# A transformer block in exact fp32: one round of norms and transposes placed ahead of its products, and the last block's attention output gathered in one place

## The chip, the cores and the metric

The kernel runs on one core of a Trainium2 chip. The metric is device time in microseconds for one launch; lower is better. TensorE (PE in the profile) multiplies, VectorE (DVE) and ScalarE (ACT) do the elementwise work, GpSimd (POOL) a few small operations, and SyncE (SP) issues most of the DMAs.

## The reference

The input is x of 2048 rows and 1024 columns. Everything is fp32.

```python
h   = layernorm(x)
q, k, v = split(h @ Wqkv + bqkv, 3)            # 256 columns each
out = softmax(q @ k.T / 16) @ v                 # one head over all 2048 rows
x   = x + layernorm(out @ Wo + bo)
h   = layernorm(x)
x   = x + layernorm((silu(h @ W_gate.T) * (h @ W_up.T)) @ W_down.T)   # inner width 2752
```

## The kernel before, in words

**Numbers.** Every fp32 operand of a large product is split into two rounded parts, hi (made by ScalarE) and lo (the rest, made by VectorE), and a product is three matmuls: hi by hi, hi by lo, lo by hi. `mm3` at L142 to L144 issues these three. `split` at L109 (ScalarE, hi) and L110 (VectorE, lo) makes the parts.

**Rows.** The 2048 rows are 16 blocks of 128 rows, numbered 0 to 15, in four groups of four. A block is loaded into one of four tiles `xin` (block t into tile t modulo 4, `load_x`, L160). `prep1` then takes the mean and variance (`norm_stats`: L116, L119 and L120 on VectorE, L121 on GpSimd), norms the rows (L127, VectorE), and turns them with eight 128-column transposes on TensorE (L135) into two PSUM banks, from where `split` writes hi and lo. Only then may the tile be loaded with the block four further on; that load is the last statement of `prep1`.

**Stage 1, products.** For each group g, `qk(g, i)` makes two slices of k (i = 0, 1) and two of q (i = 2, 3) with 24 matmuls each, in banks 4 and 5, and `v_block(g, tb)` makes 128 rows of v with eight pairs of matmuls of 512 and 256 columns (L189, L190), in bank 6 or 7. A `v_block` ends with two VectorE adds that read its bank (L193, L194) and a `split` of the result; the next but one `v_block` reuses the bank. Group 0 and the norms of blocks 4 to 7 have a hand-written order. From group 1 on the order of statements is only a wish: the program is built by a scheduler that plans every engine's order from the traced statements, their data dependencies and estimated costs, and engines run their own list in that fixed order. A few statements (`keep_in_program_order`) must stay in the traced order, among them the statistics of blocks 8 to 11. In the kernel before, `prep1` of block 8+i is traced behind `qk(1, i)`.

**Stage 2, attention.** For each block i of 128 queries: `turn` transposes the softmax weights (L396), `attend(i)` multiplies them with v, `turn_o` transposes the result (L415) and splits it (L417, L418), `proj` multiplies with Wo (12 matmuls of `mm3`, in banks 5 and 7, each bank read by L428), and `xpose` and `residual` do the second norm of an earlier block. `attend` keeps hi and lo of v side by side, so one matmul of 512 columns (L404) gives both hi by hi (left half of bank 6) and hi by lo (right half), and one of 256 columns (L405) adds lo by hi to the right half. ScalarE copies the left half out (L407), and VectorE adds the right half to the copy (L408).

**The seam.** While the last block, 15, is in attention, the feed-forward stage has begun: its products (L761) and the splits of its weights and inputs (L563, L564, L109, L110, L540, L775, on ScalarE and VectorE) are mixed in, the block's result lies in the tile `xe`, and `proj(15)` is the last of the attention. In the feed-forward stage TensorE takes weights from slots that ScalarE and VectorE refill as TensorE frees them.

Of the kernel before, what the change touches and what calls it, by code (L numbers as in the profile page):

```python
# [18 lines left out]
D = 256  # L19
F = 2752  # L20
NT = T // P
NC_ = C // P
G = 512
NG = T // G
TB = G // P
FB = F // P
FR = F - FB * P
NKB = T // P
# [6 lines left out]
def block_kernel(ctx, tc, x, wqk, wv, bqk, bv, wo, bo, wgu, wlast, wd, out):  # L35
# [12 lines left out]
    nc = tc.nc  # L48
# [4 lines left out]
    def tl(p, shape, dt, name):  # L53
        return p.tile(shape, dt, tag=name, name=name, bufs=1)
# [22 lines left out]
    bank = [tl(bank_pool, [P, 512], F32, f"bank{i}") for i in range(8)]  # L77
# [27 lines left out]
    def f32(ap):  # L105
        return ap.bitcast(F32)
# [17 lines left out]
    def norm_rows(t, pin):  # L124

        m, r, _ = norm_stats([t[:, 0:512], t[:, 512:1024]], pin)
        nc.vector.tensor_scalar(t, t, m, r, ALU.subtract, ALU.mult)  # L127

    def transpose_rows(t, dst, tb, banks):

        for hf in range(2):
            b = banks[hf]
            for j in range(4):
                cb = 4 * hf + j
                nc.tensor.transpose(b[:, j * P : (j + 1) * P], t[:, cb * P : (cb + 1) * P], ident)  # L135
            src = b.rearrange("p (j t) -> p j t", j=4)
            cols = slice(tb * P, (tb + 1) * P)
            split(dst[:, 4 * hf : 4 * hf + 4, 0, cols], dst[:, 4 * hf : 4 * hf + 4, 1, cols], src)

    def mm3(o, w, m, first, last, pin=lambda i: i):  # L140

        pin(nc.tensor.matmul(o, w[0], m[0], start=first, stop=False))  # L142
        pin(nc.tensor.matmul(o, w[0], m[1], start=False, stop=False))  # L143
        return pin(nc.tensor.matmul(o, w[1], m[0], start=False, stop=last))  # L144


    def kT(d, g):
        return slot(kx, 4 * d + g)

    vt = a1.rearrange("p a b c -> p (a b c)").rearrange("p (k h d) -> p k h d", h=2, d=D)  # L150
# [8 lines left out]
    def load_x(t):  # L159
        nc.sync.dma_start(xin[t % TB], x[t * P : (t + 1) * P, :])  # L160
# [3 lines left out]
    def prep1(t, banks):  # L164

        r = xin[t % TB]
        norm_rows(r, tc.keep_in_program_order if t < 3 * TB else None)
        transpose_rows(r, xT[(t // TB) % 2], t % TB, banks)
        if t + TB < NT:
            load_x(t + TB)  # L170

    def qk(g, i, b, pin=lambda i: i):
        xg = xT[g % 2]
        for c in range(8):
            mm3(b, (wqk_s[i][:, c, 0, :], wqk_s[i][:, c, 1, :]), (xg[:, c, 0, :], xg[:, c, 1, :]), c == 0, c == 7, pin)
        if i < 2 or g == 0:
            dst = kT(i, g) if i < 2 else qa[:, i - 2, :, :]
            pin(nc.scalar.activation(dst[:, 0, :], b, AF.Identity, bias=bqk_s[:, i : i + 1]))
            pin(nc.vector.scalar_tensor_tensor(dst[:, 1, :], b, bqk_s[:, i : i + 1], f32(dst[:, 0, :]), ALU.add, ALU.subtract))
        else:  # L180
            s = qst[i % 2]
            nc.scalar.activation(s, b, AF.Identity, bias=bqk_s[:, i : i + 1])
            nc.sync.dma_start(q_d[g][:, i - 2, :], s)

    def v_block(g, tb, b):
        xg = xT[g % 2]
        cols = slice(tb * P, (tb + 1) * P)
        for c in range(8):
            nc.tensor.matmul(b, xg[:, c, 0, cols], wv_s[:, c, :, :].rearrange("p a f -> p (a f)"), start=(c == 0), stop=False)  # L189
            nc.tensor.matmul(b[:, D:], xg[:, c, 1, cols], wv_s[:, c, 0, :], start=False, stop=(c == 7))  # L190
        k = g * TB + tb
        s = vst[tb % 2]
        nc.vector.tensor_tensor(s, b[:, :D], bv_s, ALU.add)  # L193
        nc.vector.tensor_tensor(s, b[:, D:], s, ALU.add)  # L194
        split(vt[:, k, 0, :], vt[:, k, 1, :], s)
# [168 lines left out]
    def o_of(i):  # L364

        return o_s[i % 2] if i < NT - 1 else xe[:, 0:D]
# [33 lines left out]
    def attend(i):  # L400
        b = bank[6]
        p = pT[i % 2]
        for k in range(NKB):
            nc.tensor.matmul(b, p[:, k, 0, :], vt[:, k, :, :].rearrange("p h d -> p (h d)"), start=(k == 0), stop=False)  # L404
            nc.tensor.matmul(b[:, D:], p[:, k, 1, :], vt[:, k, 0, :], start=False, stop=(k == NKB - 1))  # L405
        o = o_of(i)
        nc.scalar.copy(o, b[:, :D])  # L407
        nc.vector.tensor_tensor(o, b[:, D:], o, ALU.add)  # L408

# [55 lines left out]
    qk(0, 3, vb[3], pin)  # L465
    for g in range(1, NG):
        for i in range(4):
            qk(g, i, bank[4 + i % 2])
            if g + 1 < NG:
                prep1((g + 1) * TB + i, (bank[2 * (i % 2)], bank[2 * (i % 2) + 1]))  # L470
        if 0 < g < NG - 1:
            for tb in range(TB):
                v_block(g, tb, bank[6 + tb % 2])
# [588 lines left out]
    for i in range(NT):  # L1062
# [26 lines left out]
        if i > 0:  # L1089
            turn_o(i - 1)  # L1090
        attend(i)
        if i > 0:
            proj(i - 1)
# [126 lines left out]
```

## Time and profile before

| what | value |
|---|---|
| time, median of 3 runs | 1691.93 us (1691.12 to 1692.08) |
| the profiled execution: its own time | 1693.37 us |
| the profiled execution: span in the trace | 1691.6 us |
| TensorE busy | 1669.9 us, 99% of the span |
| VectorE busy | 1097.4 us, 65% |
| ScalarE busy | 700.8 us, 41% |
| GpSimd busy | 94.1 us, 6% |
| mean granted TensorE clock | 0.996 of full speed |

The span starts with the first instruction and ends with the last; the profiled execution's own time has 1.8 us more around it. The profile's waits give, for an instruction that found its engine idle, what released it: engine, line and tile waited for, total time, number of waits, longest wait. The chain of waits follows the last instruction back to what released it, step by step. The table of windows gives each engine's busy time in a stretch and, under PEclk, the share of its full clock that TensorE was granted there.

### The profile page before, as it was taken

Reading aid. Unit: us, or ns where it says so; the run is one execution under the profiler, and the core shown is the slowest. Engines: PE = TensorE matmul, PEld = TensorE weight load, DVE = VectorE, ACT = ScalarE, POOL = GpSimd, SP = SyncE. Lnnn points to the kernel's source line nnn. Section 1 sums busy time; section 2 is a strip of 40 time slices with the busy share of each in tenths; the row PEclk is TensorE's granted clock in tenths of the full one; section 3 lists DMA queues with packets and bytes.
Section 4 is the critical chain, followed back from the end, with each engine's and each line's share of the span. In section 5 each row is a group of like instructions: output and inputs, shape, how many; then the busy total and the mean of one; then the engine's idle time right before and its main releaser. Section 6 shows DMA issues by size and latency. Waiting matters only on the chain.

```text
span 1691.6 us, 21210 instructions
## 1 busy us (share of the span) xinstructions
PE 1669.9 (99%) x7821; PEld 1391.9 (82%) x7821; DVE 1097.4 (65%) x1676; ACT 700.8 (41%) x1043; POOL 94.1 (6%) x121
## 2 busy tenths in 40 slices
PE   9999999999999999999999999999999999999997
PEld 8888887888788888888888888888888888888886
DVE  7552667667787777776578457966555665455458
ACT  4222455544544444444355444433333333344343
POOL 1000000000001111111000000100000000000001
PEclk9999999999999999999999999999999999999999
DMA  6221023334646566666567666533322223576664
GB/s 214 72 72 57 26 88 117 99 116 174 219 166 210 197 216 228 218 210 219 175 213 249 213 192 203 199 118 119 129 102 94 94 94 125 215 217 197 191 192 159
DMA packets 131016, 271.02 MB, mean 160 GB/s; under 512 B 13280, under 2 KB 29792, under 8 KB 130912
## 3 DMA queue, kind: packets, MB, share of 16 engines
q1 hardware_dynamic: 129472, 266.52, 47.5%
q10 hardware_dynamic: 1440, 3.15, 0.5%
q8 instruction: 61, 1.00, 0.3%
q14 instruction: 43, 0.35, 0.1%
HBM read 185.73 MB, written 83.89 MB: 159 GB/s over the span
## 4 chain that ended last, share of the span: by engine, by line
PE 95%; DVE 2%; DMA 1%; issue 1%; ACT 1%; POOL 0%; POOLq 0%; SPq 0%; DVEq 0%; ACTq 0%
PE bank L761 71%; PE bank L142 4%; PE bank L143 4%; PE bank L144 4%; PE bank L404 3%; PE bank L405 2%; PE bank L396 1%; PE bank L189 1%; PE bank L503 1%; DMA f<-x 1%; PE bank L190 1%; PE bank L274 1%; DVE a L110 0%; PE bank L135 0%; PE bank L945 0%
## 5 line engine op out<-in xcount | busy, mean ns | idle before, releaser
L761 PE MATMUL bank<-a 128*128 128x512 f32 x1164 | 274.2, 389 | 0.0
L761 PEld LDWEIGHTS bank<-a 128*128 128x128 f32 x1164 | 218.5, 188 | 45.4
L761 PE MATMUL bank<-xb,a 128*128 128x512 f32 x912 | 212.3, 389 | 0.4 <-DVE a L110 0.4
L761 PEld LDWEIGHTS bank<-xb,a 128*128 128x128 f32 x912 | 171.0, 188 | 36.3 <-DVE a L110 0.8
L110 DVE TENSOR_TENSOR a<-f2p,a 128x1024 fp32r<-128x1024 f32 (+2 forms) x133 | 134.8, 1013 | 58.5 <-ACT a L109 54.5
L109 ACT CAST a<-f2p 128x1024 fp32r<-128x1024 f32 (+2 forms) x133 | 117.7, 885 | 128.6 <-PE bank L761 104.2
L110 DVE TENSOR_TENSOR a<-f,a 128x1024 fp32r<-128x1024 f32 (+2 forms) x87 | 89.8, 1033 | 113.5 <-ACT a L109 111.5
L761 PE MATMUL bank<-wvo 128*128 128x512 f32 x612 | 149.6, 389 | 0.0
L761 PE MATMUL bank<-kx,a 128*128 128x512 f32 x612 | 145.9, 389 | 0.0
L761 PE MATMUL bank<-a,a 128*128 128x512 f32 x588 | 139.6, 389 | 0.0
L761 PEld LDWEIGHTS bank<-wvo 128*128 128x128 f32 x612 | 114.9, 188 | 23.9
L761 PEld LDWEIGHTS bank<-kx,a 128*128 128x128 f32 x612 | 114.9, 188 | 23.8
L761 PEld LDWEIGHTS bank<-a,a 128*128 128x128 f32 x588 | 110.4, 188 | 22.9
L109 ACT CAST a<-f 128x1024 fp32r<-128x1024 f32 (+2 forms) x87 | 68.1, 783 | 125.1 <-PE bank L761 104.5
L775 DVE TENSOR_TENSOR p_s<-bank,p_s 128x512 f32<-128x512 f32 x96 | 65.2, 682 | 76.6 <-PE bank L761 42.4
L761 PE MATMUL bank<-a,wvo 128*128 128x512 f32 x444 | 106.0, 389 | 0.0
L761 PE MATMUL bank<-kx,wvo 128*128 128x512 f32 x420 | 100.1, 389 | 0.0
L404 PE MATMUL bank<-a,a 128*128 128x512 f32 x256 | 94.8, 403 | 2.8 <-ACT f L505 2.0
L761 PEld LDWEIGHTS bank<-a,wvo 128*128 128x128 f32 x444 | 83.3, 188 | 17.3
L110 DVE TENSOR_TENSOR wvo<-f,wvo 128x1024 fp32r<-128x1024 f32 (+1 forms) x51 | 59.6, 1169 | 55.8 <-ACT wvo L109 55.6
L761 PEld LDWEIGHTS bank<-kx,wvo 128*128 128x128 f32 x420 | 78.8, 188 | 16.4
L121 POOL TENSOR_TENSOR small<-small,mhalf 128x1 f32<-128x1 f32 x48 | 38.7, 808 | 697.2 <-DVE small L120 668.6
(267 smaller groups left out, 2782.4 us busy)
## 6 DMA issues: line engine op xcount, KB each, us to landing
f2p<-wgu SPq DMA_DIRECT2D x41, 512.0 KB, 5.2
f<-x SPq DMA_DIRECT2D x30, 512.0 KB, 3.8
hd_S<-p_s SPq DMA_DIRECT2D x60, 256.0 KB, 4.6
f<-wgu SPq DMA_DIRECT2D x22, 512.0 KB, 3.5
wr<-wgu SPq DMA_DIRECT2D x21, 512.0 KB, 5.7
f<-wd SPq DMA_DIRECT2D x20, 512.0 KB, 4.7
hd_A<-xi SPq DMA_DIRECT2D x40, 256.0 KB, 2.0
td_T<-f SPq DMA_DIRECT2D x40, 256.0 KB, 4.5
```

Source lines behind the costliest of these rows:

```text
L109: nc.scalar.copy(hi, src)
L110: (lo_engine or nc.vector).tensor_tensor(lo, src, f32(hi), ALU.subtract)
L121: nc.gpsimd.tensor_tensor(s[:, 15:16], s[:, 14:15], mhalf, ALU.pow)
L142: pin(nc.tensor.matmul(o, w[0], m[0], start=first, stop=False))
L143: pin(nc.tensor.matmul(o, w[0], m[1], start=False, stop=False))
L144: return pin(nc.tensor.matmul(o, w[1], m[0], start=False, stop=last))
L189: nc.tensor.matmul(b, xg[:, c, 0, cols], wv_s[:, c, :, :].rearrange("p a f -> p (a f)"), start=(c == 0), stop=False)
L190: nc.tensor.matmul(b[:, D:], xg[:, c, 1, cols], wv_s[:, c, 0, :], start=False, stop=(c == 7))
L404: nc.tensor.matmul(b, p[:, k, 0, :], vt[:, k, :, :].rearrange("p h d -> p (h d)"), start=(k == 0), stop=False)
L405: nc.tensor.matmul(b[:, D:], p[:, k, 1, :], vt[:, k, 0, :], start=False, stop=(k == NKB - 1))
L761: one = nc.tensor.matmul(o, w[i], m[j], start=first and n == 0, stop=last and n == 2, skip_group_check=chained)
L775: nc.vector.tensor_tensor(o, a, b, op)
```

## The change

Two parts. First, in group 1 alone, `prep1` of blocks 8 to 11 is traced in front of `qk(1, i)` and not behind it; in group 2, `prep1` of blocks 12 to 15 stays behind `qk(2, i)`. Second, `attend` of block 15 runs the three parts as three matmuls of 256 columns, all added up in the left half of bank 6, so that ScalarE's copy is the whole result and no VectorE add follows. The other 15 blocks keep the old form.

```diff
     def attend(i):
         b = bank[6]
         p = pT[i % 2]
+        o = o_of(i)
+        if i == NT - 1:
+
+            for k in range(NKB):
+                for j, (h, l) in enumerate(((0, 0), (0, 1), (1, 0))):
+                    nc.tensor.matmul(b[:, :D], p[:, k, h, :], vt[:, k, l, :], start=(k == 0 and j == 0), stop=(k == NKB - 1 and j == 2))
+            nc.scalar.copy(o, b[:, :D])
+            return
         for k in range(NKB):
             nc.tensor.matmul(b, p[:, k, 0, :], vt[:, k, :, :].rearrange("p h d -> p (h d)"), start=(k == 0), stop=False)
             nc.tensor.matmul(b[:, D:], p[:, k, 1, :], vt[:, k, 0, :], start=False, stop=(k == NKB - 1))
-        o = o_of(i)
         nc.scalar.copy(o, b[:, :D])
         nc.vector.tensor_tensor(o, b[:, D:], o, ALU.add)
...
     for g in range(1, NG):
         for i in range(4):
+            if g == 1:
+                prep1(2 * TB + i, (bank[2 * (i % 2)], bank[2 * (i % 2) + 1]))
             qk(g, i, bank[4 + i % 2])
-            if g + 1 < NG:
-                prep1((g + 1) * TB + i, (bank[2 * (i % 2)], bank[2 * (i % 2) + 1]))
+            if g == 2:
+                prep1(3 * TB + i, (bank[2 * (i % 2)], bank[2 * (i % 2) + 1]))
         if 0 < g < NG - 1:
             for tb in range(TB):
                 v_block(g, tb, bank[6 + tb % 2])
```

Here `NT` is 16, `NKB` 16, `NG` 4, `TB` 4 and `D` 256. Line numbers in the text are those of the kernel before.

## The prediction

> **What bounds the kernel now.** I read the shares first, then TensorE's waits, then the windows for the clock, then the chain around each wait.
>
> ```profile
> PE 1669.9 (99%) x7821; PEld 1391.9 (82%) x7821; DVE 1097.4 (65%) x1676; ACT 700.8 (41%) x1043; POOL 94.1 (6%) x121
> ```
>
> TensorE sets the end: it idles 21.7 us in all (1691.6 − 1669.9). So a change can win idle time, or time at a lowered clock, but hardly more. TensorE's longest waits:
>
> ```profile
> PE bank L415 <- DVE xe L408: 3.3, 1, 3.3
> PE bank L135 <- DVE f L127: 2.2, 1, 2.2
> PE bank L404 <- ACT f L505: 2.0, 2, 1.4
> ```
>
> The first lies at the seam, the second in stage 1: the two places that the diff touches. Behind 450 us the waits add up to only 0.4 us, so what is won there reaches the end. The windows around these waits show a second price:
>
> ```profile
> 99.00:105.00 6.00, 5.61 (x27) 5.14 (x28) 3.18 (x7) 1.58 (x3) 0.00 (x0) 0.72 0.26 90
> ...
> 262.00:278.00 16.00, 14.57 (x82) 12.22 (x80) 11.29 (x24) 8.21 (x15) 1.63 (x4) 1.00 0.35 92
> ...
> 442.00:450.00 8.00, 7.09 (x25) 5.74 (x26) 5.95 (x9) 4.33 (x6) 0.00 (x0) 0.79 0.93 315
> ```
>
> The clock share falls only here: 0.28 × 6 = 1.68 and 0.21 × 8 = 1.68 us lost, that is 3.4 us at half speed behind each wait. The 1.4 us wait in the middle row cost no clock.
>
> Stage 1, the chain of waits:
>
> ```profile
> 90.75 3.76 DMA f<-x
> 94.54 1.29 DVE small L116 x2
> ...
> 98.61 0.73 DVE f L127
> 99.39 1.97 PE bank L135 x8
> ```
>
> Block 11's transposes (99.39) wait for its norm. Its statistics ran at 92.20, but a little behind them block 14's sat at the head of VectorE's queue until 94.54 for a load issued at 90.75, when block 10's transposes freed the tile. From 99.39 to 102.82 TensorE did eight transposes (0.87) and five matmuls of `v_block` (3 × 0.235 + 2 × 0.115), 1.81 us of work in 3.43. The wait costs 2.19 + 1.62 = **3.8 us**.
>
> The seam, in the timeline:
>
> ```profile
> 439.24 0.39 PE L144 MATMUL bank<-wvo,oTs 128*128 128x512 f32 x1
> 439.54 0.36 ACT L407 COPY xe<-bank 128x256 f32<-128x256 f32 x1
> ...
> 442.44 0.42 DVE L408 TENSOR_TENSOR xe<-bank,xe 128x256 f32<-128x256 f32 x1
> ...
> 442.91 0.44 PE L415 MATMUL bank<-ident,xe 128*128 128x128 f32 x2 [3.29 <-DVE xe L408]
> ```
>
> ScalarE's copy is done at 439.90; the add starts 2.54 us later, because VectorE has feed-forward splits and sums back to back ahead of it.
>
> **What the Trainium skill says.** "TensorE: Matmul & The Clock Gate", section "What's actually happening": the clock is halved or full, judged in a free-running window of 3413 ns. The two losses of 3.4 us at half clock agree. The same page, "Why this matters for your kernels", asks for no idle gap over about 3 us; here 2.19 us sufficed, and 1.4 us did not, and between these I take a chance. "Perfetto Trace Analysis", section "Tensor Engine Instruction (MATMUL, LD_WEIGHTS)": ScalarE and VectorE queues are strictly first in, first out; the 2.54 us of the ready add agree. "TensorE: Matmul & The Clock Gate", "Back-to-back issue gap": spacing is set by weight load and matmul together; for my 256-column matmuls the trace has a row of its own, below.
>
> **Part 1, the moved `prep1`.** I compared both kernels' built instruction orders, engine by engine. Nothing is added or removed. Block 8's transposes move from behind the 14th matmul of `qk(1,2)` to behind that of `qk(1,1)`, block 9's from `qk(1,3)` into `qk(1,2)`, block 10's from behind `v_block(2,0)` to before the last pair of `v_block(1,2)`. With 0.227 us per 512-column matmul, 0.35 per `v_block` pair and 0.87 per eight transposes, I place the new order on the trace:
> - Block 8 at 64.34 + 14 × 0.227 = 67.5 (73.0 before), block 9 at 73.0 (79.1). `qk(1,3)` ends at 82.6 as before; 3 pairs, then block 10 at 83.7 (89.7).
> - Block 14's load goes out 1.06 us behind block 10's start, as before: 84.7; landing takes 3.79 to its reader: 88.5 (94.5 before).
> - TensorE: block 10's transposes, the last pair of `v_block(1,2)`, `v_block(1,3)`, block 12's transposes, `v_block(2,0)` reach 91.35. There `v_block(2,1)` needs bank 7, which `v_block(1,3)` filled and VectorE must have read (L194).
> - VectorE's new order has block 14's statistics ahead of that read: 88.52 + statistics 1.20 + L193 0.33 + L119 0.11 + split 0.60 + split 0.33 + L119 0.11 + split 0.60 + L194 0.42 = 92.22.
>
> So a **new wait of 0.9 us** comes at 91.35; behind it stand `v_block(2,1)`, `v_block(2,2)` and block 11's transposes, which then come at 97.5, 3.4 us after their norm (94.1), and no longer wait. The clock should hold, as it did at 1.4 us. Won: 3.8 − 0.9 = **2.9 us**. If the load takes 0.5 us more or less, the wait follows it by as much until VectorE's earlier work (done 88.1) sets it: at least 0.5.
>
> The rest of part 1 costs nothing, for these covers: GpSimd's powers (0.55 us) come as often, with the engine 6% busy. On SP, the loads of blocks 12, 13 and 14 pass before the q stores and the read-back of q (L369 at 85.62), which VectorE takes up only at 133.3; if that cover were gone, a store's 2 us would appear there. `v_block(3,0)` moves back from 101 to about 153, but the orders are the same again from block 2's `attend` (about 219) on. TensorE's waits between 105 and 219 sum to 1.5 us (0.7, 0.5 and 0.3, for ScalarE, VectorE, ScalarE). I take no change, with bounds of −1.5 and +1.5.
>
> **Part 2, block 15.** TensorE runs 48 matmuls of 256 columns for 16 pairs. Stage 1 has such matmuls, each behind its own weight load:
>
> ```profile
> 15.46 2.87 PE bank L274 x24
> ```
>
> 0.12 us each, so 5.76 for 16 × 0.35 = 5.60: +0.16 us. The add (0.33 of VectorE's time) goes. L415 follows the copy: 439.95, not 442.91. Next come two transposes (0.22) and six products (1.37), to 441.55. Then `proj(15)` must have bank 7, which L428 reads for `proj(14)`, and L428 stands in VectorE's queue where it stood, less the add: 442.77 − 0.33 + 0.75 = 443.19. The stall is not gone; **what is late next is L428**, and TensorE waits 1.65 us there, `proj(15)` and all feed-forward products behind it. The third matmul needs L418, done 443.52, in time. `proj(15)` runs 443.22 to 445.95 at full clock; before, the products behind it began at 448.90. Won: **2.95 us**, of which 1.6 is clock. The +0.16 is hidden behind VectorE's queue; without that cover it is paid. Bounds: if 1.65 us of idling costs the clock, 1.7 less; if VectorE is less behind, up to 1.6 more.
>
> **Sum.** 2.9 + 2.95 = 5.9 us off the profiled execution: span 1685.7, own time 1687.5. The median of the runs is 1.4 below that own time, so 1691.93 − 5.9 = 1686.0.
>
> **Rivals.**
> - *The clock still drops at the seam.* 1.65 us is 48% of a window, and with part of the 0.5 us ahead of it up to 2.0 us (59%) can fall into one; 1.4 us (41%) was safe, 2.19 us (64%) was not. 5.9 − 1.7 = 4.2: 1687.7.
> - *The wait in stage 1 only changes place.* Block 14's load lands 1.3 us later (it now runs with the q stores): 2.2 us of idling and a clock drop take part 1 whole. Then 1689.0. Against it: the loads issued at 74.05, 80.19 and 90.75 were in their readers' hands 3.5 to 3.8 us later.
> - *Slower.* The same wait at `v_block(2,1)`, VectorE held at its head by block 14's load. The change loses once wait and clock exceed the 6.75 us of 3.8 and 2.95, a wait of 5.1 us, a load 4.2 us late. At 8 us late, 1695.8. For it: two q stores, the read-back and the load crowd into 83 to 89 us. Against it: DMA was busy for only 0.41 of 75 to 90 with nearly the same transfers.
> - *The change does nothing*, the scheduler keeping its order: excluded by the built orders.
> - *More than computed*: the waits of 105 to 219 go too: 1684.5.
>
> **How the numbers follow.** A measurement can tell 0.2% (3.4 us) from no change. As computed 0.5 (1686.0, own range 1684.8 to 1687.2), clock drop at the seam 0.25 (1687.7), wait moved 0.13 (1689.0, within 0.2%), more 0.07, slower 0.05, of which 0.01 stays within 0.2%. Faster 0.5 + 0.25 + 0.07 = 0.82, same 0.14, slower 0.04. Range 1684.2 to 1689.6: the extra gain below, the moved wait above.
>
> **What would show it.** In the changed profile: no wait of L135 for L127; one of about 0.9 us of L189 for L194 near 91; L415 waiting under 0.6 us for ScalarE's copy; the first matmul of `proj(15)` waiting about 1.7 us for L428 or L418; PEclk at 1.00 near 99 and 442. I am wrong if the waits behind 105 us grow by more than 2, or the feed-forward stage shows new ones.

## The result, and the profile after

| kernel | median of its runs | ratio to the kernel before, 95% interval |
|---|---|---|
| before | 1692.03 us (14 runs) | |
| changed | 1688.33 us (1686.61 to 1689.32, 14 runs) | 0.9977 [0.9970, 0.9984] |

The change makes the kernel 3.7 us faster. The forecast said 1686.0, that is 5.9 us. The profiled execution of the changed kernel took 1688.38 us of its own time, with a span of 1686.6.

Line numbers below are those of each run's own kernel. In the changed kernel they are 7 to 9 higher than before: L435 is the old L428 (the read of a `proj` bank), L437 the store of `proj`'s result, L594 the old L585 (loads of feed-forward inputs), L676 the load of weights, L770 the old L761 (feed-forward products), and L831 the old L822, ScalarE's copy of a feed-forward bank into the tile `xi`. L422 and L425 are the old L415 and L418 (block 15's transposes and the split of their result), L572 and L573 the old L563 and L564 (input splits), and L408 is the new line of block 15's 256-column matmuls.

The shares, after:

```profile
PE 1666.8 (99%) x7837; PEld 1389.7 (82%) x7837; DVE 1096.0 (65%) x1675; ACT 698.8 (41%) x1043; POOL 93.7 (6%) x121
```

TensorE is busy for 3.1 us less than in the first profile and idle for 19.8 us instead of 21.7. The busy time that went is the lowered clock, which the windows over the two old places show as gone (the columns are the stretch, its length, busy time of PE, PEld, DVE, ACT and POOL, then PEclk, the DMA share and GB/s):

```profile
99.00:105.00 6.00, 6.00 (x29) 4.97 (x28) 5.21 (x12) 1.21 (x3) 0.55 (x1) 1.00 0.29 90
...
442.00:450.00 8.00, 8.00 (x37) 6.61 (x36) 3.47 (x4) 2.36 (x3) 0.00 (x0) 1.00 0.81 287
```

TensorE's waits, after:

```profile
PE bank L142 <- DVE f L435: 1.5, 1, 1.5
...
PE bank L770 <- ACT xi L831: 1.4, 1, 1.4
...
PE bank L189 <- DVE small L120: 0.4, 1, 0.4
```

Neither the 3.3 us nor the 2.2 us of before is there. The first and third lines are the waits that the forecast put in their place. (For the third it named L194. The profile names L120, which VectorE runs directly behind L194: L194 ended at 91.68, and TensorE went on at 91.83.) The second line is a wait for which the forecast had no price: it lies at 457 us, in the feed-forward stage.

The seam in TensorE's timeline (start, duration, line and operation; the bracket gives the idle time ahead and what ended it):

```profile
433.37 1.35 PE L408 MATMUL bank<-a,a 128*128 128x256 f32 x10
434.56 0.40 PE L142 MATMUL bank<-wvo,oTs 128*128 128x512 f32 x1
...
436.03 0.44 PE L422 MATMUL bank<-ident,xe 128*128 128x128 f32 x2
...
439.41 0.47 PE L142 MATMUL bank<-wvo,oTs 128*128 128x512 f32 x1 [1.53 <-DVE f L435]
...
442.25 1.52 PE L770 MATMUL bank<-qa,a 128*128 128x512 f32 x6
```

Ten 256-column matmuls take 1.19 us, so 0.119 each. The transposes of the result (L422) start with no wait. The products behind `proj(15)` start at 442.25 instead of 448.90: 6.65 us ahead, of which only 5.0 us are left at the end of the span. The chain of waits behind the seam shows where the rest went (start, duration, what):

```profile
438.60 0.66 DVE f L435
...
439.29 7.60 DMA at_d<-f
...
446.91 0.32 SPq L594
...
447.80 5.04 DMA f<-wgu
...
456.74 0.58 ACT xi L831
...
457.37 2.83 PE bank L770 x11
```

VectorE writes `proj(14)` into the tile f4[0] (L435). Its store takes 7.6 us to land. At the head of SP's queue an input load into the same tile (L594) waits for that store, and the weights' load stands behind it in the queue. ScalarE splits these weights when they land (452.94), then, in its own order, runs one more split of weights and two of inputs, and only then copies the bank that TensorE needs. TensorE became free sooner than this chain.

### The profile page after: what moved, and what is told of

It is laid out like the page before. It is cut to its first block, busy times and chain, and to the rows that moved or that the text cites. A ratio compares the mean times of both kernels' runs of the same rounds, so it can differ in the third digit from the quotient of the medians.

```text
span 1686.6 us, 21240 instructions
## 1 busy us (share of the span) xinstructions
PE 1666.8 (99%) x7837; PEld 1389.7 (82%) x7837; DVE 1096.0 (65%) x1675; ACT 698.8 (41%) x1043; POOL 93.7 (6%) x121
## 4 chain that ended last, share of the span: by engine, by line
PE 93%; DMA 2%; DVE 2%; ACT 1%; issue 1%; POOL 0%; SPq 0%; POOLq 0%; DVEq 0%; ACTq 0%
PE bank L770 70%; PE bank L142 4%; PE bank L143 4%; PE bank L144 4%; PE bank L412 3%; PE bank L413 2%; PE bank L396 1%; PE bank L189 1%; PE bank L512 1%; DMA f<-x 1%; PE bank L274 1%; PE bank L190 1%; DMA out<-bo_s 0%; DMA at_d<-f 0%; DVE a L110 0%
## 5 line engine op out<-in xcount | busy, mean ns | idle before, releaser
L770 PE MATMUL bank<-a 128*128 128x512 f32 x1164 | 274.3, 389 | 0.0
L770 PEld LDWEIGHTS bank<-a 128*128 128x128 f32 x1164 | 218.6, 188 | 45.3
L770 PE MATMUL bank<-xb,a 128*128 128x512 f32 x912 | 212.5, 390 | 0.4 <-DVE a L110 0.4
L770 PEld LDWEIGHTS bank<-xb,a 128*128 128x128 f32 x912 | 171.0, 188 | 36.1 <-DVE a L110 0.8
L110 DVE TENSOR_TENSOR a<-f2p,a 128x1024 fp32r<-128x1024 f32 (+2 forms) x133 | 134.7, 1012 | 58.1 <-ACT a L109 51.2
L109 ACT CAST a<-f2p 128x1024 fp32r<-128x1024 f32 (+2 forms) x133 | 117.5, 883 | 129.2 <-PE bank L770 104.7
L110 DVE TENSOR_TENSOR a<-f,a 128x1024 fp32r<-128x1024 f32 (+2 forms) x87 | 89.7, 1031 | 112.7 <-ACT a L109 110.7
L770 PE MATMUL bank<-wvo 128*128 128x512 f32 x612 | 149.6, 389 | 0.0
L770 PE MATMUL bank<-kx,a 128*128 128x512 f32 x612 | 145.9, 389 | 0.0
L770 PE MATMUL bank<-a,a 128*128 128x512 f32 x588 | 139.8, 390 | 1.4 <-ACT xi L831 1.4
L770 PEld LDWEIGHTS bank<-wvo 128*128 128x128 f32 x612 | 114.9, 188 | 23.8
L770 PEld LDWEIGHTS bank<-kx,a 128*128 128x128 f32 x612 | 114.9, 188 | 23.8
L770 PEld LDWEIGHTS bank<-a,a 128*128 128x128 f32 x588 | 110.3, 188 | 24.6 <-ACT xi L831 1.8
L109 ACT CAST a<-f 128x1024 fp32r<-128x1024 f32 (+2 forms) x87 | 67.9, 780 | 129.7 <-PE bank L770 106.2
L770 PE MATMUL bank<-a,wvo 128*128 128x512 f32 x444 | 106.0, 389 | 0.0
L770 PE MATMUL bank<-kx,wvo 128*128 128x512 f32 x420 | 100.1, 389 | 0.0
L770 PEld LDWEIGHTS bank<-a,wvo 128*128 128x128 f32 x444 | 83.4, 188 | 17.3
L110 DVE TENSOR_TENSOR wvo<-f,wvo 128x1024 fp32r<-128x1024 f32 (+1 forms) x51 | 59.6, 1168 | 55.8 <-ACT wvo L109 55.7
L770 PEld LDWEIGHTS bank<-kx,wvo 128*128 128x128 f32 x420 | 78.8, 188 | 16.3
L412 PE MATMUL bank<-a,a 128*128 128x512 f32 x240 | 88.8, 403 | 2.8 <-ACT f L514 2.1
```

The costliest lines, as they stand in the source:

```text
L109: nc.scalar.copy(hi, src)
L110: (lo_engine or nc.vector).tensor_tensor(lo, src, f32(hi), ALU.subtract)
L770: one = nc.tensor.matmul(o, w[i], m[j], start=first and n == 0, stop=last and n == 2, skip_group_check=chained)
```

## The experiments

Two theories at the start. **T:** this chain of transfers caps what the seam can win. **R:** each part fell short by itself. The kernel before ran beside every group of variants; its medians were 1692.19, 1691.85 and 1692.36 us. The groups ran on different chips, so variants of different groups are compared only roughly, to about 0.5 us.

### The changed kernel again

> The changed kernel once more, for a second profiled execution beside the variants on one chip: 1688.3 by every theory. If the waits of the first trace are systematic, the wait for the copy of xi is 1.0 to 1.7 us again and the one at the first matmul of proj(15) 1.4 to 1.7 us; if they are chance, they are not.

Measured: 1688.56 us, 0.9980 [0.9972, 0.9988]. Both waits came back, the one for L435 with 1.3 us, the one for the copy of `xi` with 0.9, both a little under the ranges given. The chain was the same. In this execution the store landed in 6.3 us instead of 7.6 and the weights' load went out at 446.79, 1.0 us sooner, but took 0.9 us longer to land. So the copy was done only 0.13 us sooner, and most of the shorter wait is TensorE's coming 0.28 us later.

### Each part alone

Part 1 alone drops the new branch in `attend`. Part 2 alone puts `prep1` back behind `qk`.

> Part 1 alone: the moved norms and transposes, block 15's attention output in its old form. Theory T (a chain of transfers behind the seam caps what part 2 wins): part 1 carries most of the gain of 3.7 us, so 2.9 to 3.2 us below the kernel before, about 1689.0; no wait for the norm near 99 us, a wait of 0.4 us for VectorE's read of a bank near 91, and the old wait of 3.3 us at the seam with TensorE's clock lowered there. Rival R (both parts fell short alike, each worth about six tenths of its forecast): 1.8 us below, about 1690.2.

> Part 2 alone: block 15's output as 48 products of 256 columns in one place, stage 1 as before. T: the seam's wait shrinks to about 1.5 us and the clock holds there, but a wait of 1 to 1.5 us for ScalarE's copy of xi comes in the feed-forward stage, because the weights' load goes out behind the store of block 14 as before; 0.5 to 1 us below the kernel before, about 1691.3. R (each part worth six tenths of its forecast): 1.8 us below, about 1690.2, and the wait in the feed-forward stage has another cause. The forecast's own sum: 2.95 us below, about 1689.1.

Measured: part 1 alone 1690.75 us, ratio 0.9988 [0.9982, 0.9995], 1.4 us below before by the medians (2.0 by the ratio). Part 2 alone 1690.84 us, 0.9992 [0.9986, 0.9999], 1.35 us below. T missed part 1 by half, and R's number was closer there; for part 2 the measured gain lies between T's 0.5 to 1 and R's 1.8. The intervals, about 1.1 us to either side, don't tell whether the parts add up to the 3.7 us of both together. The windows of the two profiles show one reason for the smaller gain of part 1. Part 1 alone, over the seam:

```profile
430.00:455.00 25.00, 21.46 (x92) 17.47 (x91) 15.27 (x19) 10.97 (x16) 0.00 (x0) 0.93 0.79 273
```

Part 2 alone, over stage 1's old wait and over the seam:

```profile
96.00:103.00 7.00, 5.08 (x34) 4.31 (x33) 5.58 (x14) 2.37 (x5) 1.06 (x2) 1.00 0.43 148
...
430.00:455.00 25.00, 22.83 (x113) 18.81 (x113) 16.10 (x20) 11.39 (x17) 0.00 (x0) 1.00 0.84 295
```

The second fence is the point: the old wait of stage 1 is still there (TensorE idle for 1.92 of 7 us), but the clock held at 1.00. The 1.62 us of lowered clock that the forecast counted at this place are paid in some executions only. Both profiles also show the wait for ScalarE's copy of `xi` in the feed-forward stage, 0.6 us in part 1 alone and 1.0 in part 2 alone. In part 2 alone its chain runs through the store of block 14 and the blocked load, as in the changed kernel. In part 1 alone it does not: the blocked load was out at 445.96, and the weights' load went out at 447.39, when VectorE had read the old weights out of the same tile (L110, done at 447.37).

### The clock: a second profile of before

> A second profiled execution of the kernel before. If both losses of clock in its first profile are systematic, the granted clock is lowered near 99 us and near 444 us again. If the loss at a wait of 2 us depends on how the wait falls into the clock's windows, this execution may show one of them or none: by the clocks of the runs so far, that near 444 us in about three of four executions, that near 99 us in about one of three. Where the clock holds near 99, the five products of v_block behind the wait take 1.8 us, not 3.4.

Measured: 1692.12 us. TensorE's waits in the two places:

```profile
PE bank L135 <- DVE f L127: 2.1, 1, 2.1
PE bank L415 <- DVE xe L408: 3.2, 1, 3.2
PE bank L761 <- ACT xi L822: 0.7, 1, 0.7
```

and its windows over both places:

```profile
96.00:104.00 8.00, 5.89 (x38) 4.99 (x37) 6.00 (x17) 2.75 (x6) 1.06 (x2) 1.00 0.41 131
440.00:450.00 10.00, 8.84 (x33) 7.16 (x34) 7.93 (x11) 4.75 (x6) 0.00 (x0) 0.83 0.85 296
```

The two old waits are the same as in the first profile, but with one loss of clock instead of two, and the execution took 1.25 us less. And there is a third wait, which the first profile did not have: 0.7 us for the copy of `xi`, although the seam is as long as ever. So this wait was in the kernel before already, in one of two profiled executions. Its chain starts elsewhere:

```profile
448.12 1.14 DVE wvo L110
449.27 0.02 issue
449.28 7.79 DMA f<-wgu
```

VectorE's read of the old weights releases the load of the new ones; the blocked load had gone out before, at 447.83. In the first profile it was the same: blocked load 449.66, read done 450.99, weights' load 451.06. There the load landed in 6.7 us and the copy was done 0.3 us before TensorE came.

Each loss of clock moves a run's mean clock by about 0.001. Over all 91 runs of before beside the variants, 30 had a mean clock of 0.998 or more (the level of the profiles with no loss), 43 had 0.997 (one loss, as here) and 18 had 0.996 or less (two, as in the first profile). Part 2 alone, which keeps only stage 1's wait, was at 0.997 or less in 7 of 21 runs; part 1 alone, which keeps only the seam's, in 16 of 21; the changed kernel in 1 of 28. So stage 1's wait seems to lose the clock in about a third of the executions, the seam's in about three quarters. The counts are rough, because a run's clock is given to 0.001 only and the idle end of the span lowers it too: before's own counts make 0.87 losses a run, not the 1.1 of these two shares. The runs' times agree that losses come and go: the 18 runs average 1693.85 us, the 43 average 1692.09, the 30 average 1691.35.

The Trainium skill ("TensorE: Matmul & The Clock Gate", "What's actually happening") has the clock judged in free-running windows. That fits: a wait of 2 us can lie in one window or across two. It is not shown, for no run shows where the windows begin. A plain limit on the length fits the five profiles of stage 1's wait as well: it lost the clock at 2.19 us and held it at 2.11, 2.02, 1.92 and 1.88.

### The weights' load ahead of the blocked load

```diff
-    for f, r in zip(order[8:], (f4[0], f4[2])):
-        f.load(r)
...
     feed.pump()
+    with tc.issue_after(wload[-1].ins):
+        for f, r in zip(order[8:], (f4[0], f4[2])):
+            f.load(r)
```

`wload` collects the weight loads that `Pair.load` issues; the last two pairs of input loads are queued behind them.

> The changed kernel with the last two pairs of input loads (into the tiles f4[0] and f4[2]) queued on SP behind the two weight loads instead of ahead of them, so that the weight loads no longer stand behind a load that waits for the store of block 14. T: the weights land near 450 us instead of 452.9, the wait of 1.35 us for the copy of xi falls to under 0.3 us, and the time falls by 1.0 to 1.4 us against the changed kernel: about 1687.1. R (the wait has another cause, such as ScalarE's own order): the wait stays, 1688.3. The input loads come later by 1 us or so; if they set the copy instead, the gain is under 0.5 us.

> The changed kernel with the weight loads first, again, on the same chip as the two others: 1687.0 by T, 1.2 to 1.5 us below the changed kernel, the wait for the copy of xi under 0.3 us; 1688.4 if the first five runs were chance.

Measured: 1687.09 us, 0.9968 [0.9956, 0.9981], and on another chip 1687.61, 0.9970 [0.9960, 0.9981]. The means are 1687.2 us over these 13 runs and 1688.5 over 28 of the changed kernel, which ran in other groups: about 1.3 us won, as T said. SP's queue in the first of them:

```profile
444.96 0.33 SPq L676 DMA_DIRECT2D f<-wgu  x1
446.10 0.35 SPq L676 DMA_DIRECT2D f2p<-wgu  x1
446.54 0.47 SPq L594 DMA_DIRECT2D f<-xs_d  x1
```

The weights go out at 444.96 instead of 447.80, and no wait for the copy of `xi` stands in TensorE's list. In the second profile 0.7 us of it was left, more than the 0.3 expected. The edit had also changed ScalarE's order: in both profiles an input split, which waits for its own later load, and a split of further weights, which waits for VectorE, stand ahead of the copy. In the second the weights (451.2) and those inputs came 0.5 and 0.7 us later, which was enough to make the copy late. So this edit alone does not tell the load's time from ScalarE's order; the last two experiments do.

> Control: the kernel before with the weight loads queued ahead of the last two pairs of input loads, and nothing else. T (the chain of transfers limits only once the seam has become shorter): the kernel before had some 0.3 us of slack there, and the wait appears only in executions in which TensorE's clock holds at the seam, about a quarter of them, so 0 to 0.4 us below the kernel before, about 1691.9. R (that order of loads is better by itself, whatever the seam does): 1.2 us below, about 1691.0.

Measured: 1691.41 us, ratio 1.0000 [0.9992, 1.0008]. The same order of loads brings the kernel before nothing that can be told from zero. By the times alone R is not quite out, for its 1.2 us (0.9993) lies just inside the interval. The trace says why nothing was won: the weights' load went out at 449.09, 7.49 us behind the store of block 14, exactly as far behind it as in the second profile of before (449.28 behind 441.79). VectorE's read sets that moment there, not the load ahead in the queue. In the changed kernel the same read was done some 3.5 us before the weights' load went out (444.34 against 447.80). So the blocked load became the limit only with the shorter seam, which is T's point, though not through the slack that T gave as the reason. The wait for `xi` was gone here, since the load landed in 3.9 us, but one of 0.8 us for VectorE's L110 came later, behind 475 us.

> Part 2 alone with the weight loads first. T: the wait of 1.0 us for the copy of xi goes, so 1.0 to 1.3 us below part 2 alone and 2.5 to 2.8 us below the kernel before, about 1689.6: part 2's gain as it leaves the seam. R (part 2 is worth no more than it showed alone): no faster than part 2 alone, 1690.8.

Measured: 1690.25 us, 0.9991 [0.9982, 0.9999], where part 2 alone had 0.9992, with an interval that holds both forecasts. The wait for `xi` was still 1.2 us in its profile. Its chain:

```profile
446.74 6.85 DMA f<-wgu
...
457.48 0.17 ACT a L109
...
459.05 0.49 ACT xi L829
```

Here the load was issued 2.3 us sooner than in part 2 alone (449.02), but took 6.85 us to land instead of 5.8, and here too the split of further weights (L109), which waits for VectorE, stands ahead of the copy. The edit moves more than one thing; T's forecast that the wait goes did not come, and the run settles no more than that.

### A longer store

```diff
         if i >= EARLY:
-            nc.sync.dma_start(at_d[i], a)
+            nc.sync.dma_start(at_d[i], a); i == NT - 2 and nc.sync.dma_start(at_d[0], a)
```

> The changed kernel with one transfer added: the store of block 14's result is issued twice, the second into a block of the scratch tensor that nothing reads. T: the input load into f4[0] must wait for both stores, so it goes out 1 to 2 us later, the second weight load behind it (one of the two now stands ahead of it) lands near 454 to 455, and the wait for the copy of xi grows from about 1.2 us to 2 to 3 us: 0.6 to 2 us above the changed kernel, 1689.0 to 1690.4. R (transfers here are covered, the wait is of ScalarE's own making): the changed kernel's 1688.4.

Measured: 1687.38 us, 0.9973 [0.9963, 0.9984]: about 1 us *faster* than the changed kernel, against both theories. SP's queue:

```profile
439.63 0.90 SPq L437 DMA_DIRECT2D at_d<-f  x2
...
444.69 0.33 SPq L676 DMA_DIRECT2D f<-wgu  x1
448.05 0.32 SPq L594 DMA_DIRECT2D f<-xs_d  x1
```

The blocked load did go out later (448.05 instead of 446.91). But with one more store in its plan the scheduler had put the first weight load ahead of it, at 444.69. My expectation took the second weight load for the critical one; it is the first. The run is not the test that was meant, but it is the cleanest test of the load's part. ScalarE's order is that of the changed kernel: the two splits of weights, the two of inputs, the copy. The load went out 3.1 us sooner and landed about 1.1 us sooner (ScalarE's first split began at 451.79 instead of 452.94), the copy was done 1.15 us sooner, and the wait for `xi` is gone, with 1.5 us of waiting at the seam as before.

### One input split later

```diff
-            for f in order[2:6]:
-                f.use()
+            for f in order[2:5]: f.use()
...
-    turned = turn_o(NT - 1, pin)
+    turned = turn_o(NT - 1, pin); order[5].use()
```

This takes 1.22 us of VectorE's work out of the queue ahead of L435.

> As the kernel with the weight loads first, and besides it one split of an input block (kx, 1.22 us on VectorE, 1.05 us on ScalarE) traced behind block 15's transposes instead of ahead of them, so that VectorE comes 1.2 us sooner to the read that frees bank 7 for proj(15). T: the wait of 1.5 us at the first matmul of proj(15) falls to 0.3 to 0.5 us, and with the weights out of the way the gain reaches the end: another 1.0 us, about 1686.1. R: with weights first or not, what is won at the seam is lost in the feed-forward stage: no faster than the kernel with the weights first, or than the changed kernel.

> The changed kernel with the one split of kx traced behind block 15's transposes, and the loads as they were, the input loads ahead of the weights. T: proj(15) starts about 0.8 us sooner (the wait for bank 7 falls from 1.5 to 0.7 us), but the weights go out no sooner than the store of block 14 lands, itself up to 1.2 us sooner; so 0 to 0.8 us below the changed kernel, 1687.5 to 1688.3, with the wait for the copy of xi still 1 us or more. R (only the seam counts): 0.8 us below, and no wait there over 0.5 us.

> The changed kernel with the split of kx behind block 15's transposes, again, beside the variant with the weights first on one chip. If the 1685.5 us of its first five runs holds: 2.5 to 3 us below the changed kernel; if those were a lucky few, 1686.5 to 1687.5. The first trace had no wait for the copy of xi; T says that ScalarE's new order there (the copy of the late weights behind the input splits) is why, so again none over 0.3 us.

Measured: with the weights first 1686.91 us, 0.9967 [0.9955, 0.9980], about the same as weights first alone, as R said; the seam's wait was 0.7 us there. Without that edit 1685.48 us, 0.9964 [0.9952, 0.9977], and again 1686.16, 0.9965 [0.9953, 0.9978], on one chip with weights first at 1687.61. The mean of these ten runs, 1686.05 us, is 2.5 us below the changed kernel and the **best version** found. T expected 0 to 0.8 us here, R 0.8, and both were too low. In the second of the two profiles TensorE's waits between 430 and 475 us are one line:

```profile
PE bank L142 <- DVE f L435: 0.3, 1, 0.3
```

There the seam's wait fell from 1.5 to 0.3 us, and with L435 came the store of block 14, the blocked load (445.22) and the weights' load (446.78, 1.0 us sooner). In the first profile the seam's wait was still 1.2 us, and yet the wait for `xi` was gone too. ScalarE in that execution:

```profile
450.68 1.05 ACT L109 CAST a<-f2p 128x1024 fp32r<-128x1024 f32 x1 [4.63 <-DMA at_d<-xe]
451.68 2.00 ACT L572 CAST a<-f 128x1024 fp32r<-128x1024 f32 x2
454.19 1.06 ACT L109 CAST a<-f 128x1024 fp32r<-128x1024 f32 x1 [0.50 <-DMA f<-wgu]
455.15 0.57 ACT L831 COPY xi<-bank 128x512 f32<-128x512 f32 x1
```

The late weights came later than in the changed kernel (their split began at 454.19 instead of 452.94), and still the copy was done at 455.7 instead of 457.3, before TensorE came at 456.15. The other splits now stand ahead of the split of the late weights, and only that one is left between it and the copy. So here ScalarE's order alone took the wait away. Together with the longer-store run, in which only the load's time had changed, this shows both terms of the wait: when the weights land, and how much work ScalarE has put between them and the copy (3.8 us in the changed kernel, 1.0 here). Shortening either is enough.

## Why the prediction was right in kind and 2.3 us off in size

**The new wait of part 1: right.** Forecast 0.9 us at `v_block(2,1)`, released by VectorE behind L194; measured 0.4 to 1.2 us in nine profiled executions that have part 1, mean 0.77. Block 14's load went out at 84.65 (forecast 84.7) and its statistics began at 88.07 (forecast 88.5). The waits between 105 and 219 us are 1.4 us, forecast 1.5.

**The seam: right.** Late next was L435 (the old L428), with 1.53 us against 1.65, and the clock held: the rival of a clock drop at the seam did not come in either profile of the changed kernel. The rivals of a moved wait, of a late load and of a larger gain did not come either.

**First step that failed:** "Behind 450 us the waits add up to only 0.4 us, so what is won there reaches the end." A wait of 0.4 us says how much TensorE waited, not how much slack its releasers had. The trace of before held the warning: the weights landed so late that ScalarE's copy was done only 0.3 us before TensorE came for it. And the 0.4 us were one execution's: the second profile of before has the wait for the copy with 0.7 us. In the changed kernel it was 1.35 us (0.9 in the second profile). The text named this as what would prove it wrong, but did not price it.

**Second step that failed:** the sum's last line, "The median of the runs is 1.4 below that own time, so 1691.93 − 5.9 = 1686.0". The 5.9 us held 3.2 us for both losses of clock (1.62 and 1.6), because the one profiled execution had both. The median run has one. Taken by the counts above, they are worth 1.62 × 1/3 + 1.6 × 3/4 = 1.75 us. The 1.4 us between that execution and the median are about this surplus (the 18 runs with two losses lie 1.7 us above the mean of all 91), and it was taken off a second time.

The sum, mended: 5.9 − 1.45 (clock) − 1.35 (copy of `xi`) + 0.5 (the wait in stage 1 was 0.4 in that profile, not 0.9) = 3.6 us; measured 3.7. So close an agreement is partly luck. By the run times of before, all losses together are worth only 0.8 us (1692.2 for all 91 runs, 1691.35 for those with none), and the sum would then be 2.7. For the parts, with the same shares and the first profile of before: part 1 wins 1.6 us of waiting (2.1 − 0.5) and 0.5 of clock less 0.6 for the copy of `xi`, 1.5 us, measured 1.4. Part 2 wins 1.7 us of waiting and 1.2 of clock less 1.0 for `xi` and 0.6 for a wait of L422 for ScalarE's copy, which the changed kernel's profile doesn't have: 1.3 us, measured 1.35.

**Luck in the number.** The measured 1688.33 lies outside the sum's own range, 1684.8 to 1687.2. It lies inside the outer range, 1684.2 to 1689.6, but only because the upper end was set for the moved wait, a rival that did not come.

## What to carry to other kernels

Before a gain is carried to the end, follow the releasers of the *next* stage back to where they start, DMA queue included, and ask how much slack each had, and which of them moves with the change. Here a load at the head of a queue that waits for an older store held the load behind it. In the kernel before that cost nothing, because VectorE released the second load later still; once VectorE came sooner, it was the limit. And a loss of clock in one profiled execution need not come in the next. Let a second profile or the clocks of the runs say how often it falls, count it with that frequency, and don't take it off a median that never had it.

## What the runs showed that I had not expected

A wait of 1.9 to 2.2 us in stage 1 cost the clock in one of five profiled executions, the one with the longest wait, and one of 3.2 to 3.5 us at the seam in four of four; a wait of 1.2 to 1.6 us there in none of eight. A load of 512 KB that went out 3 us sooner landed only 1 us sooner in the longer-store run and 2 us sooner with the weights first. And an added store of 512 KB made the kernel faster: with it the scheduler's order of the queue changed, and the weights' load passed the blocked one.
